# A dense layer's combined weights: made one stage earlier, and the layer's leading pair of tiles by seven block products

## The chip, the cores and the metric

The kernel runs on one core of a Trainium2 chip. That core has a matrix engine (TensorE, PE in the profile), a vector engine (VectorE, DVE), a scalar engine (ScalarE, ACT), a general one (GpSimd, POOL), and a queue engine (SyncE, SP), which issues every DMA of this kernel. Each works through its own list of instructions in order and waits for others on semaphores. The metric is the device time of one execution in microseconds, lower is better, as the median of several executions without the profiler.

## The reference

All data are float32. The input x has two batches of 1024 rows of 1024 numbers. Four residual layers follow one another, each on the layer-normed x:

```
x = x + attn_a(layernorm(x))     # 32 heads, rope, causal, an adapter of 10 keys, output projection w_proj
x = x + ffn(layernorm(x))        # dense 1024x1024 + 8 gated low-rank experts
x = x + attn_b(layernorm(x))     # 8 heads over 1024 keys, not causal, output projection
x = x + ffn(layernorm(x))        # the same dense layer and weights again
```

The dense layer is where the change lies:

```
base_out = x @ W_base.T + b_base
weights  = sparsemax(x @ W_router.T + b_router)        # 8 numbers per row
h        = x @ lora_A                                   # 8 experts x 16
out      = base_out + (h * weights) @ lora_B
```

## The kernel before

A tile is 128 rows of x. A product of two tiles of rows with a 1024x1024 weight can be made plainly, by 32 matmuls of 128x128 by 128x512 (two tiles, two halves of the columns, eight blocks of the inner dimension), or by Strassen's way in Winograd's form: the pair of tiles is one 2x2 matrix of blocks, the weight another, and seven products of blocks take the place of eight. Seven products of four matmuls each are 28. For this the weight's blocks b11, b12, b21, b22 must be combined beforehand (L1294, `combine_weights`): (3) = b22-b12, (2) = (3)+b11, (4) = (2)-b21, and b12 itself is overwritten by b12-b11. Each is a set of four 128x512 pieces, c = 0 to 3. Three sets are kept in DRAM (`tf`) and streamed back through a ring of four places while the layer runs, in the order 2, 3, 4 for every pair of tiles (`piece`, L1238).

The order of the PE's instructions is written out by Python generators, each of which yields after every matmul; the SP's order is written out as well in this part of the kernel. DVE, ACT and POOL are ordered by a scheduler that uses its own costs. Small jobs for the DVE can be put into a queue of chores (`fill.chore`): one is emitted after each matmul, and `fill.flush` emits the rest of a key, with all that stands before it in the queue.

The part of the kernel that the change touches, in the order of time:

1. `proj_a(1, ...)` (L1102): the output projection of the first attention for batch 1, four pairs of tiles, each by seven products (`seven_added`, L1049; products in the order 1, 6, 2, 7, 5, 4, 3, into two PSUM banks that take turns). During it the dense layer's weights are loaded, three DMAs at a time (`each`, L1638). In the last pair the first two tiles of the dense layer are fetched and normalized ahead (`then.prepare()`).
2. `f1_0 = f1(0)`, which is `ffn(b=0, k=0, ...)` (L1201): the first dense layer on batch 0, again four pairs. For each pair: eight transposes per tile (`turn`), `hidden` (16 matmuls of 136 columns per pair, followed on the DVE by the router, `router`, L1241, some 26 small instructions), then the dense product, in whose middle the gated hidden values are transposed (`turned`, L1283, tiles `ht_f` and `hwT`).
3. The first pair of f1_0 is made by `plain` (L1310). Meanwhile `combine_weights` makes the twelve combined pieces on the DVE, in eight places that later serve as ring and work room (`qkb_f`, `kqb_f`), and stores each to `tf`; four more subtractions overwrite b12 ("wb1"). At the end of the pair four pieces are read back into the ring. Pairs 2 to 4 are made by seven products.

The first pair of one later call, `ffn(0, 1, ...)` with `late_room`, is also made by `plain`; that stays.

Of the kernel before, what the change touches and what calls it, by code (L numbers as in the profile page):

```python
# [147 lines left out]
def tile_model(ctx: ExitStack, tc: tile.TileContext, d, out: bass.AP):  # L148
# [950 lines left out]
        return {1: a[11], 2: a[12], 3: a[12], 4: a[22], 5: s1, 6: s2, 7: a[21]}  # L1099


    def proj_a(b, big, wp, tile_of, then=None, each=None):  # L1102

        yts, xs, stores = {}, {}, deque()
        count = {"yt": 0, "x": 0}

        def take(kind, shape, name):
            count[kind] += 1
            return tile_of(kind, count[kind] - 1, shape, name)

        def fetch(p):
            for t in (2 * p + 1, 2 * p):
                yts[t] = take("yt", [P, NG, P], f"yt{b}_{t}")
                for g in range(NG):
                    sp.dma_start(yts[t][:, g, :], yd[b, g][:, t * P : (t + 1) * P])

        def fetch_x(p):
            for t, n in ((2 * p, 0), (2 * p + 1, 1), (2 * p + 1, 0), (2 * p, 1)):
                xs[t, n] = take("x", [P, HF], f"xp{b}_{t}_{n}")
                sp.dma_start(xs[t, n], d["x"][b, t * P : (t + 1) * P, n * HF : (n + 1) * HF])  # L1120

        def store(t, n):
            stores.append((x1[b, t][:, n * HF : (n + 1) * HF], xs.pop((t, n))))
            if len(stores) > 1:
                sp.dma_start(*stores.popleft())

        if not wp:
            for i in range(2):
                wp[i] = big.tile([P, 4, C], F32, tag="h16", name=f"wp{i}")
                for g in range(4):  # L1130
                    sp.dma_start(wp[i][:, g, :], d["w_projT"][(4 * i + g) * P : (4 * i + g + 1) * P, :])
            for i, tag in ((3, "wqk"), (2, "wqk"), (4, "wv")):
                wp["T", i] = big.tile([P, 4, HF], F32, tag=tag, name=f"wpt{i}")
        b11, b12, b21, b22 = (wp[i][:, :, n * HF : (n + 1) * HF] for i in range(2) for n in range(2))
        right = {1: b11, 2: b21, 3: b22, 4: wp["T", 4], 5: b12, 6: wp["T", 2], 7: wp["T", 3]}
        fetch(0)
        fetch_x(0)
        yield READY
        for p in range(NT // 2):
            if then is not None and p == NT // 2 - 1:  # L1140
                then.prepare()
            if p + 1 < NT // 2:
                fetch(p + 1)
            if each is not None:
                each()
            if b == 0 and p == 0:

                for c in range(4):
                    for dst, op, x, y in ((7, pin_sub, b22, b12), (6, pin_add, right[7], b11), (4, pin_sub, right[6], b21)):
                        fill.chore("wp", lambda c=c, dst=dst, op=op, x=x, y=y: op(right[dst][:, c], x[:, c], y[:, c]))  # L1150
                for t in (1, 0):
                    yt = yts.pop(t)
                    for n in range(2):
                        op = next_bank([P, HF], f"op{b}_{t}_{n}")
                        for g in range(NG):
                            mm(op, lhsT=yt[:, g, :], rhs=wp[g // 4][:, g % 4, n * HF : (n + 1) * HF],
                               start=(g == 0), stop=(g == NG - 1))
                            yield HF * COL
                        x = xs[t, n]
                        dve.tensor_add(x, op, x)  # L1160
                        store(t, n)
                    if t == 1:
                        fetch_x(p + 1)
                for c in range(4):
                    fill.chore("wp1", lambda c=c: pin_sub(b12[:, c], b12[:, c], b11[:, c]))
                continue
            nm = f"p{b}_{p}"
            a = {10 * i + j: yts.pop(2 * p + i - 1)[:, 4 * j - 4 : 4 * j] if j == 2 else yts[2 * p + i - 1][:, 4 * j - 4 : 4 * j]
                 for i in (1, 2) for j in (1, 2)}
            left = left_factors(a, *(tile_of("s", i, [P, 4, P], f"s{i}_{nm}") for i in range(2)), nm)  # L1170
            flush = {6: ("wp", nm), 5: ("wp1",)}
            ends = {11: (2 * p, 0), 12: (2 * p, 1), 21: (2 * p + 1, 0), 22: (2 * p + 1, 1)}

            def ready(i):
                for key in flush.get(i, ()):
                    fill.flush(key)
                if i == 2:
                    while stores:
                        sp.dma_start(*stores.popleft())
                    if p + 1 < NT // 2:  # L1180
                        fetch_x(p + 1)
                    elif then is not None:
                        then.prepare()
                if i == 5:
                    if each is not None:
                        each()
                    if then is not None and p == NT // 2 - 1:
                        then.prepare()

            yield from seven_added(nm, left, right, [tile_of("sum", i, [P, HF], f"sum{i}_{nm}") for i in range(2)],  # L1190
                                   {i: xs[at] for i, at in ends.items()}, lambda i: store(*ends[i]), ready)
        sp.dma_start(*stores.popleft())
        yield ("proj", b)
# [2 lines left out]

    tf = {(i, c): dram.tile([P, HF], F32, name=f"tf{i}_{c}") for i in (2, 3, 4) for c in range(4)}

    kept = [{}, {}, {}]

    def ffn(b, k, src, dst, w, wk, tiles, places, free=lambda: True, there=lambda t: True):  # L1201

        tiles = list(tiles)
        first = (b, k) == (0, 0)
        late_room = (b, k, tiles[0]) == (0, 1, 0)

        seq = [t for p in range(0, len(tiles), 2) for t in (tiles[p + 1], tiles[p])]
# [73 lines left out]
        def turned(p):  # L1283
# [4 lines left out]
                flip(tp[:, i, :], hws.pop(t).rearrange("p e r -> p (e r)"), ident)  # L1288
            hwT = wk.tile([P, 4, P], F32, tag="hwT", name=f"hwT_f{b}_{k}_{e}", bufs=1)
            act.copy(hwT[:, :2], tp)  # L1290
            if p or not (first or late_room):
                act.activation(hwT[:, 2], tp[:, 1], AF.Copy, scale=-1.0)
                dve.tensor_sub(hwT[:, 3], hwT[:, 0], hwT[:, 1])
            return hwT  # L1294

        def combine_weights(slots):
            b11, b12, b21, b22 = (w["wb"][:, 4 * i : 4 * i + 4, n * HF : (n + 1) * HF] for i in range(2) for n in range(2))
            ts = {}

            def make(i, c, op, x, y):  # L1300
                t = ts[i, c] = slots[len(ts) % len(slots)]
                op(t, x, y)
                sp.dma_start(tf[i, c], t)

            for c in range(4):
                fill.chore("wb", lambda c=c: make(3, c, pin_sub, b22[:, c], b12[:, c]))
                fill.chore("wb", lambda c=c: make(2, c, pin_add, ts[3, c], b11[:, c]))
                fill.chore("wb", lambda c=c: make(4, c, pin_sub, ts[2, c], b21[:, c]))

        def plain(p):  # L1310
            order = [(n, c) for n in range(2) for c in range(NC)]
            order = order[:4] + order[NC:] + order[4:NC]
            for i in range(2):
                t = seq[2 * p + i]
                ops = {}
                for n, c in order:
# [3 lines left out]
                    op = ops[n]  # L1320
                    mm(op, lhsT=xts[t][:, c, :], rhs=w["wb"][:, c, cols], start=(c == 0), stop=False)
                    yield HF * COL
                    if late_room and (n, c) == (0, 3):

                        pin_add(xs[t][:, HF:], op, xs[t][:, HF:])
                    if (i, n, c) == (0, 0, 3):
                        normalize(2)
                    if late_room and (i, n, c) == (1, 0, 1):
                        while stores:
                            sp.dma_start(*stores.popleft())  # L1330
                        fetch(3)
                    if (i, n, c) == ((1, 1, 5) if late_room else (0, 1, 3)):
                        normalize(3)
                    if i and c == 5:
                        yield from turn(2, (1 - n,))
# [6 lines left out]
                    store(t, n)  # L1342
                    yield HF * COL
            yield from transposed(xns[seq[3]], place_xt(3), f"f{b}_{k}_{seq[3]}", by=(next_bank, next_bank))
            fill.flush("wb")
            if first:
                b11, b12 = (w["wb"][:, :4, n * HF : (n + 1) * HF] for n in range(2))
                for c in range(4):
                    fill.chore("wb1", lambda c=c: pin_sub(b12[:, c], b12[:, c], b11[:, c]))

        def take_room():
            if not room:
                ring, work, more = places()
                room.update(ring=ring, work=work, x=more[:, :2].rearrange("p a c -> p (a c)"),
                            xt=more[:, 2:].rearrange("p a (b c) -> p (a b) c", c=P))
            if not first:
                for c in range(4):
                    piece(2, c)

        fetch(0)  # L1360
        fetch(1)
# [10 lines left out]
        for p in range(n_pairs):  # L1372
# [4 lines left out]
                sp.dma_start(*stores.popleft())  # L1377
            if last:
                yield AHEAD
            plainly = p == 0 and (first or late_room)  # L1380
            if not plainly:
                ring, work = room["ring"], room["work"]
                a = {10 * i + j: xts[t][:, 4 * j - 4 : 4 * j] for i, t in ((1, e), (2, o)) for j in (1, 2)}
# [7 lines left out]
                    if i != 3 or not late_room:  # L1391
                        fetch(i)
            if plainly:
                if first:
                    combine_weights([room[kind][:, c] for kind in ("ring", "work") for c in range(4)])
                yield from plain(p)
                if late_room:
                    while not free():
                        yield WAIT
                    take_room()  # L1400
                else:
                    for c in range(4):
                        piece(2, c)
                continue
            fill.chore(nm, lambda a=a: pin_sub(a[21], a[11], a[21]))
            b11, b12, b21, b22 = (w["wb"][:, 4 * i : 4 * i + 4, n * HF : (n + 1) * HF] for i in range(2) for n in range(2))
# [172 lines left out]
    with tc.manual_schedule(engines={mybir.EngineType.PE}):  # L1579
        with tc.tile_pool(name="big", bufs=2, side="left", reuse_waits="tile") as bigp:  # L1580
# [54 lines left out]
                    return big.tile(shape, F32, tag={"yt": "t4k", "x": "tt"}[kind], name=name)  # L1635
                return pj.tile(shape, F32, tag=kind, name=name)

            fill.add(Dense(lambda: proj_a(1, big, wp, place, f1_0, lambda: load(3))))  # L1638
            fill.drain()
            assert not loads  # L1640
            own.close()
# [105 lines left out]
```

## Time and profile before

| | us |
|---|---|
| median of three executions without the profiler | 2433.34 (2433.07 to 2435.3) |
| the profiled execution, device time | 2443.13 |
| its span, first to last instruction | 2441.4 |
| PE busy in the span | 2377.8 |
| last pair of proj_a(1) on the PE (L198, x_p to z_p) | 1436.72 to 1460.75 |
| transposes of f1_0's first two tiles (L204) | from 1460.75 |
| f1_0: first matmul of `hidden` for pair 1 / pair 2 / pair 3 / pair 4 | 1462.96 / 1506.16 / 1539.56 / 1572.71 |

Times within a trace are microseconds from the start of the span. In a timeline line the first number is the start, the second the length of a merged stretch, x the number of instructions in it. A float32 matmul stands as two records (two passes), so 8 records are one product of four matmuls. Names such as y_p, z_p, x_f are the PSUM banks of the products: _p of the projection, _f of the dense layer; fo_f are the banks of `plain`.

### The profile page before, as it was taken

Reading aid. Unit: us, or ns where it says so; the run is one execution under the profiler, and the core shown is the slowest. Engines: PE = TensorE matmul, PEld = TensorE weight load, DVE = VectorE, ACT = ScalarE, POOL = GpSimd, SP = SyncE. Lnnn points to the kernel's source line nnn. Section 1 sums busy time; section 2 is a strip of 40 time slices with the busy share of each in tenths; the row PEclk is TensorE's granted clock in tenths of the full one; section 3 lists DMA queues with packets and bytes.
Section 4 is the critical chain, followed back from the end, with each engine's and each line's share of the span. In section 5 each row is a group of like instructions: output and inputs, shape, how many; then the busy total and the mean of one; then the engine's idle time right before and its main releaser. Section 6 shows DMA issues by size and latency. Waiting matters only on the chain.

```text
span 2441.4 us, 60572 instructions
## 1 busy us (share of the span) xinstructions
PE 2377.8 (97%) x25147; PEld 1084.3 (44%) x25147; DVE 1429.7 (59%) x4310; ACT 1100.3 (45%) x2104; POOL 591.6 (24%) x927
## 2 busy tenths in 40 slices
PE   8999999999999999999999999999999999989999
PEld 4435443455344544445433444574333643233454
DVE  6576666666656666666741236567666766553453
ACT  2346655666565666566642000013345446654200
POOL 1432222222323223222211131202111112121332
PEclk9999999999999999999999999999999999999999
DMA  4443423333233333333212654532323202123543
GB/s 149 139 131 109 135 88 131 97 93 109 99 111 114 93 97 92 97 97 114 84 62 79 219 182 141 163 123 82 109 87 105 90 25 96 66 95 100 173 156 121
DMA packets 173044, 271.56 MB, mean 111 GB/s; under 512 B 16224, under 2 KB 76768, under 8 KB 172768
## 3 DMA queue, kind: packets, MB, share of 16 engines
q1 hardware_dynamic: 172768, 267.68, 34.2%
q8 instruction: 197, 3.23, 0.5%
q14 instruction: 79, 0.65, 0.1%
HBM read 212.05 MB, written 55.57 MB: 110 GB/s over the span
## 4 chain that ended last, share of the span: by engine, by line
PE 86%; DVE 9%; DMA 2%; ACT 2%; issue 1%; POOL 0%; SPq 0%; DVEq 0%; POOLq 0%
PE st L394 9%; PE sc L322 8%; PE y_A L416 5%; PE y L200 5%; PE y_f L198 4%; PE z L200 4%; PE st L392 3%; PE z_f L198 3%; PE x L200 3%; PE y_v L200 3%; PE x_f L198 3%; PE y_B L416 2%; PE y_f L200 2%; PE y_p L198 2%; DVE pr_A L335 2%; PE x_v L200 2%
## 5 line engine op out<-in xcount | busy, mean ns | idle before, releaser
L506 ACT ACTIVATE pt<-st 128x1024 f32<-128x1024 f32 (+1 forms) x418 | 425.9, 1019 | 615.5 <-PE st L394 484.4
L343 ACT ACTIVATE pr_A<-pr_A,nmax_A 128x896 f32<-128x896 f32 (+7 forms) x512 | 389.9, 765 | 55.1 <-DVE nmax_A L335 54.6
L335 DVE CUSTOM_DVE_ANT_0 pr_A<-sc,mask 128x512 f32<-128x512 f32 (+3 forms) x512 | 251.4, 537 | 193.7 <-PE st L394 92.2
L322 PE MATMUL sc<-kT,qT 32*128 32x512 f32 (+3 forms) x1536 | 328.0, 523 | 3.5 <-DVE part_A L335 1.7
L394 PE MATMUL st<-qT,kT 32*128 32x512 f32 (+3 forms) x1536 | 307.8, 488 | 0.0
L335 DVE CUSTOM_DVE_ANT_0 pr_A<-sc,mask,part_A 128x512 f32<-128x512 f32 (+1 forms) x256 | 156.2, 647 | 147.5 <-PE sc L322 96.7
L401 POOL TENSOR_SCALAR_AFFINE_SELECT pt<-pt 128x256 f32<-128x256 f32 x256 | 106.0, 432 | 470.5 <-ACT pt L506 470.5
L343 ACT ACTIVATE pr_B<-pr_B,nmax_B 128x1024 f32<-128x1024 f32 x128 | 145.6, 1140 | 51.6 <-DVE nmax_B L335 51.6
L239 POOL TENSOR_TENSOR xf<-xf,b_base 128x256 f32<-128x256 f32 x100 | 72.9, 761 | 378.4 <-DVE xn_f L261 330.1
L322 PE MATMUL sc<-kq,qk 32*128 32x512 f32 x512 | 146.8, 650 | 14.1 <-DVE nmax_B L335 9.4
L416 PE MATMUL y_A<-pt,v 128*32 128x512 f32 (+3 forms) x1536 | 158.6, 501 | 0.0
L394 PE MATMUL st<-rows_B,kq 32*128 32x512 f32 x512 | 145.0, 643 | 2.0 <-ACT pt L506 1.4
L394 PEld LDWEIGHTS st<-qT,kT 32*128 32x128 f32 x1536 | 133.8, 185 | 16.6 <-issue 11.6
L392 PE MATMUL st<-rows_A,ones 3*128 3x512 bf16 (+3 forms) x768 | 127.8, 329 | 5.5 <-DVE nmax_A L335 5.0
L335 DVE CUSTOM_DVE_ANT_0 pr_B<-sc,zeros 128x512 f32<-128x512 f32 x128 | 83.3, 687 | 72.4 <-PE sc L322 72.3
L335 DVE CUSTOM_DVE_ANT_0 pr_B<-sc,zeros,part_B 128x512 f32<-128x512 f32 x128 | 91.0, 747 | 58.4 <-PE sc L322 58.4
L392 PEld LDWEIGHTS <-ones 3*128 3x128 bf16 x768 | 36.8, 91 | 196.1 <-issue 188.8
L322 PEld LDWEIGHTS sc<-kT,qT 32*128 32x128 f32 x1536 | 113.5, 184 | 17.9 <-issue 5.9
L830 POOL TENSOR_TENSOR qr<-qr,sin 128x256 f32<-128x256 f32 x64 | 60.5, 945 | 221.5 <-DVE qr L826 220.5
L343 ACT ACTIVATION_READ_ACCUMULATOR pr_A<-pr_A,nmax_A 128x1 f32 x512 | 97.1, 190 | 0.0
L200 PE MATMUL y<-tt,wqk 128*32 128x512 f32 x768 | 92.6, 594 | 0.0
L416 PEld LDWEIGHTS y_A<-pt,v 128*32 128x32 f32 x1536 | 33.8, 109 | 119.9 <-issue 109.2
(429 smaller groups left out, 4227.0 us busy)
## 6 DMA issues: line engine op xcount, KB each, us to landing
tt<-td SPq DMA_DIRECT2D x252, 256.0 KB, 2.8
qkb_f<-tf SPq DMA_DIRECT2D x84, 256.0 KB, 3.0
qkb_s<-tf SPq DMA_DIRECT2D x84, 256.0 KB, 3.1
wqk<-in_w_attnT SPq DMA_DIRECT2D x32, 512.0 KB, 5.2
xf<-x SPq DMA_DIRECT2D x25, 512.0 KB, 4.1
xa<-in_x SPq DMA_DIRECT2D x16, 512.0 KB, 6.0
wv<-in_w_attnT SPq DMA_DIRECT2D x8, 1024.0 KB, 5.4
yd<-ys SPq DMA_DIRECT2D x32, 256.0 KB, 2.7
```

What stands on the lines that cost most here:

```text
L198: return pe.matmul(out, lhsT=lhsT, rhs=rhs, start=start, stop=stop, skip_group_check=True)
L200: pe.matmul(out[i : i + 32], lhsT=lhsT[:, i : i + 32], rhs=rhs, start=start, stop=stop, skip_group_check=True)
L239: pool.tensor_add(dst[:, i : i + 2 * P], a[:, i : i + 2 * P], b[:, i : i + 2 * P])
L322: yield w * COL, lambda: pe.matmul(dst[:, o : o + w], lhsT=self.qt[rows, qc : qc + P], rhs=self.kt[rows, c0 : c0 + w], start=True, stop=True)
L335: minimum[0] = dve.tensor_tensor_reduce(pr[:, c0 : c0 + w], sc[:, i, o : o + w], m, -self.scale, BIG if c0 == 0 else self.part[:, col], AL ...
L343: tc.keep_in_program_order(act.activation(pr[:, :nk], pr[:, :nk], AF.Exp, bias=self.nmax[:, col], scale=-1.0, accum_out=self.sums[:, col]))
L392: yield w * COL / 4, lambda: pe.matmul(dst[:, o : o + w], lhsT=of["ones"][three, :], rhs=self.rows[three, off : off + w], start=True, stop ...
L394: yield w * COL, lambda: pe.matmul(dst[:, o : o + w], lhsT=self.kt[rows, kb * P : (kb + 1) * P], rhs=rhs, start=self.extra, stop=True)
L401: pool.affine_select(out=dg, in_=dg, compare_op=ALU.is_ge, fill=0.0, base=0, pattern=[[0, 2], [1, P]], channel_multiplier=-1)
L416: pe.matmul(self.y[32 * h : 32 * h + 32, off : off + w], lhsT=self.value(h, kb), rhs=pt[h // 2][:, h % 2, o : o + w], start=self.opens, st ...
L506: act.activation(pt[:, :, low_:wide_], st[:, :, low_:wide_], AF.Exp, scale=ts[0][0].scale)
L830: pool.tensor_mul(qr[:, hs], qr[:, hs], sin[:, cols][:, hs])
```

## The change

`combine_weights` becomes a function of its own beside `ffn`, and is called from proj_a(1) at the head of the last pair, through a new argument `meanwhile`. The outstanding store of x is issued first, and four places of the pool that holds the projection's x are taken (`tw0` to `tw3`). The twelve combined pieces pass through these four places in turn, each stored to `tf` from there, so that from the fifth on a piece waits until the store of the one four before it has landed. The four subtractions into b12 follow as chores "wb1". All sixteen stand in the chore queue ahead of the last pair's own left factors, and are emitted by the time of product 6.

In `ffn`, the case `first` is gone: f1_0's leading pair is made by seven products like the others. The ring is filled at its start (`take_room` now issues four reads of `tf` before the pair's own fetches of the tiles of pair 2). `plain` is left for `late_room` alone.

```
@@ proj_a
-    def proj_a(b, big, wp, tile_of, then=None, each=None):
+    def proj_a(b, big, wp, tile_of, then=None, each=None, meanwhile=None):
...
             if each is not None:
                 each()
+            if meanwhile is not None and p == NT // 2 - 1:
+
+                while stores:
+                    sp.dma_start(*stores.popleft())
+                meanwhile([take("x", [P, HF], f"tw{i}") for i in range(4)])
             if b == 0 and p == 0:
...
+    def combine_weights(slots, w):
+
+        b11, b12, b21, b22 = (w["wb"][:, 4 * i : 4 * i + 4, n * HF : (n + 1) * HF] for i in range(2) for n in range(2))
+        ts = {}
+
+        def make(i, c, op, x, y):
+            t = ts[i, c] = slots[len(ts) % len(slots)]
+            op(t, x, y)
+            sp.dma_start(tf[i, c], t)
+
+        for c in range(4):
+            fill.chore("wb", lambda c=c: make(3, c, pin_sub, b22[:, c], b12[:, c]))
+            fill.chore("wb", lambda c=c: make(2, c, pin_add, ts[3, c], b11[:, c]))
+            fill.chore("wb", lambda c=c: make(4, c, pin_sub, ts[2, c], b21[:, c]))
+        for c in range(4):
+            fill.chore("wb1", lambda c=c: pin_sub(b12[:, c], b12[:, c], b11[:, c]))
+
@@ ffn
         tiles = list(tiles)
-        first = (b, k) == (0, 0)
         late_room = (b, k, tiles[0]) == (0, 1, 0)
...
-            if p or not (first or late_room):
+            if p or not late_room:
                 act.activation(hwT[:, 2], tp[:, 1], AF.Copy, scale=-1.0)
                 dve.tensor_sub(hwT[:, 3], hwT[:, 0], hwT[:, 1])
             return hwT
...
@@ plain
             yield from transposed(xns[seq[3]], place_xt(3), f"f{b}_{k}_{seq[3]}", by=(next_bank, next_bank))
-            fill.flush("wb")
-            if first:
-                b11, b12 = (w["wb"][:, :4, n * HF : (n + 1) * HF] for n in range(2))
-                for c in range(4):
-                    fill.chore("wb1", lambda c=c: pin_sub(b12[:, c], b12[:, c], b11[:, c]))
...
@@ take_room
-            if not first:
-                for c in range(4):
-                    piece(2, c)
+            fill.flush("wb")
+            for c in range(4):
+                piece(2, c)
...
-            plainly = p == 0 and (first or late_room)
+            plainly = p == 0 and late_room
...
             if plainly:
-                if first:
-                    combine_weights([room[kind][:, c] for kind in ("ring", "work") for c in range(4)])
                 yield from plain(p)
-                if late_room:
-                    while not free():
-                        yield WAIT
-                    take_room()
-                else:
-                    for c in range(4):
-                        piece(2, c)
+                while not free():
+                    yield WAIT
+                take_room()
                 continue
...
-            fill.add(Dense(lambda: proj_a(1, big, wp, place, f1_0, lambda: load(3))))
+            fill.add(Dense(lambda: proj_a(1, big, wp, place, f1_0, lambda: load(3),
+                                       lambda slots: combine_weights(slots, w))))
```

More of the change, by code (lines that the diff above doesn't have):

```diff
@@ L1294, in turned @@
             return hwT
[L1296 to L1303, printed above, removed]
-            for c in range(4):
-                fill.chore("wb", lambda c=c: make(3, c, pin_sub, b22[:, c], b12[:, c]))
-                fill.chore("wb", lambda c=c: make(2, c, pin_add, ts[3, c], b11[:, c]))
-                fill.chore("wb", lambda c=c: make(4, c, pin_sub, ts[2, c], b21[:, c]))
         def plain(p):
@@ L1322, in plain @@
                     yield HF * COL
-                    if late_room and (n, c) == (0, 3):
+                    if (n, c) == (0, 3):
                         pin_add(xs[t][:, HF:], op, xs[t][:, HF:])
@@ L1327, in plain @@
                         normalize(2)
-                    if late_room and (i, n, c) == (1, 0, 1):
+                    if (i, n, c) == (1, 0, 1):
                         while stores:
@@ L1331, in plain @@
                         fetch(3)
-                    if (i, n, c) == ((1, 1, 5) if late_room else (0, 1, 3)):
+                    if (i, n, c) == (1, 1, 5):
                         normalize(3)
@@ L1393, in ffn @@
             if plainly:
-                if first:
-                    combine_weights([room[kind][:, c] for kind in ("ring", "work") for c in range(4)])
                 yield from plain(p)
-                if late_room:
-                    while not free():
-                        yield WAIT
-                    take_room()
-                else:
-                    for c in range(4):
-                        piece(2, c)
+                while not free():
+                    yield WAIT
+                take_room()
                 continue
```

## Prediction

> **What bounds the kernel now.** I read the page's busy times first, then the PE's timeline over the two stages that change, then the granted clock there, then the DVE's and POOL's timelines, last the DMAs. The page:
>
> ```profile
> span 2441.4 us, 60572 instructions
> PE 2377.8 (97%) x25147; PEld 1084.3 (44%) x25147; DVE 1429.7 (59%) x4310; ACT 1100.3 (45%) x2104; POOL 591.6 (24%) x927
> ```
>
> The PE is the bound: what leaves its list or its waits leaves the time. The PE's timeline, from the projection's last product through f1_0's first pair to the starts of `hidden` for pairs 2, 3 and 4:
>
> ```profile
> 1457.32 3.60 PE L198 MATMUL z_p<-wp,yt 128*128 128x512 f32 x8
> 1460.75 1.04 PE L204 MATMUL xt_f<-ident,xn_f 128*128 128x128 f32 x8
> 1462.96 3.87 PE L198 MATMUL hp_f<-la,xt_f 128*128 128x136 f32 x32
> 1466.67 8.75 PE L198 MATMUL fo_f<-wb,xt_f 128*128 128x512 f32 x20
> 1477.83 0.69 PE L204 MATMUL ht_f<-ident,hs_f 128*128 128x128 f32 x2 [2.42 <-DVE hs_f L1267]
> 1478.31 3.20 PE L198 MATMUL fo_f<-wb,xt_f 128*128 128x512 f32 x4
> ...
> 1487.45 8.85 PE L198 MATMUL fo_f<-wb,xt_f 128*128 128x512 f32 x20 [0.78 <-DVE xf L1341]
> ...
> 1504.83 1.09 PE L204 MATMUL xt_f<-ident,xn_f 128*128 128x128 f32 x8 [0.78 <-DVE xf L1341]
> 1506.16 2.12 PE L198 MATMUL hp_f<-la,vm_f 128*128 128x136 f32 x16 [0.24 <-ACT xt_f L234]
> ...
> 1539.56 2.02 PE L198 MATMUL hp_f<-la,xt_f 128*128 128x136 f32 x16
> ...
> 1572.71 3.87 PE L198 MATMUL hp_f<-la,xt_f 128*128 128x136 f32 x32
> ```
>
> From `hidden` to `hidden`, the plain pair takes 1506.16 - 1462.96 = 43.20, the pairs by seven products 33.40 (to 1539.56) and 33.15 (to 1572.71). Eight records of 512 columns take 3.43 from start to start (1457.32 to 1460.75), so one matmul is 0.858. The four records at 1478.31 took 3.04 until the next group at 1481.35, where 1.72 is usual: the clock was down behind the idle 2.42. The same place by stretches of four us (span, busy PE, PEld, DVE, ACT, POOL, then granted clock, DMA share, GB/s):
>
> ```profile
> 1472.00:1476.00 4.00, 3.41 (x8) 1.15 (x7) 4.00 (x13) 0.00 (x0) 2.83 (x4) 1.00 0.05 18
> 1476.00:1480.00 4.00, 2.17 (x4) 1.16 (x5) 4.00 (x10) 0.60 (x3) 0.96 (x1) 0.69 0.40 149
> 1480.00:1484.00 4.00, 4.00 (x10) 1.79 (x9) 2.85 (x7) 0.18 (x1) 0.04 (x1) 0.88 0.68 249
> ```
>
> The DVE is full from 1472 to 1480 and the clock sags after the PE's gap. On the DVE, the router's small steps (they end in `hs_f`, which the PE waits for) stand between the twelve combinations; and a combination that meets POOL takes 1.07 where 0.69 is usual. The DVE's line before that is from the projection's last pair:
>
> ```profile
> 1443.86 0.69 DVE L227 TENSOR_TENSOR sum_p<-sum_p,y_p 128x512 f32<-128x512 f32 x1 [4.16 <-PE y_p L198]
> ...
> 1474.18 1.07 DVE L224 TENSOR_TENSOR kqb_f<-wb 128x512 f32<-128x512 f32 x1
> ...
> 1475.30 1.08 DVE L227 TENSOR_TENSOR kqb_f<-kqb_f,wb 128x512 f32<-128x512 f32 x1
> ```
>
> ```profile
> 1473.17 3.79 POOL L239 TENSOR_TENSOR xf<-xf,b_base 128x256 f32<-128x256 f32 x4 [12.36 <-DVE xn_f L261]
> ```
>
> And the DMAs, issue to landing (KB each, median us), within 1395 to 1515:
>
> ```profile
> x<-xp SPq DMA_DIRECT2D x13, 256.0 KB, 3.2
> xf<-x SPq DMA_DIRECT2D x5, 512.0 KB, 4.3
> tf<-qkb_f SPq DMA_DIRECT2D x8, 256.0 KB, 2.0
> ```
>
> **The change part by part.** *The leading pair by seven products.* The plain pair's 43.20 becomes that of a pair by seven products: 33.15 or 33.40 in the rows, I take 33.3, so **-9.9** (ends -10.05 and -9.8). Of 10.05, four matmuls fewer are 4 x 0.858 = 3.43; the idle 2.42 and the 1.32 of low clock behind it are 3.74; two waits of 0.94 for bank reads by the DVE at L1341 and 0.45 of transposes that nothing covers at the pair's end are 2.3; the rest, 0.6, is smaller gaps. The added copies, sums, the third and fourth hwT block and the POOL additions are in the 33.3 already, since pairs 2 to 4 have them. The seven products need their left sums at product 6; in the changed DVE list these come directly after the transposes' copies, some 5 us ahead.
>
> *Sixteen DVE instructions in the projection's last pair.* At 0.60 from start to start, they are 9.6. Between 1440 and 1460 the DVE was busy 9.7 of 20, so they fit, but just. I walked the changed DVE list: four of them run right after 1437.6, the rest from the sum of product 6 (1443.75, PE's end of y_p) on, with one or two between any two instructions that the PE waits for. By 0.60 a step I get the read of x_p's bank at 1449.1 (product 5 wants it at 1450.45), the sum of product 7 at 1452.5 (product 4 wants its bank at 1453.89), product 3's left factor at about 1456 (wanted at 1457.32), the first normalized tile at 1457.7 (wanted 1460.75) and the second between 1460 and 1461.5 (wanted 1461.8 by its transposes). The last has next to no margin, and POOL's pieces decide it: six pieces of POOL's additions run among these sixteen. DVE additions beside POOL that read a PSUM bank kept their 0.69 (1454.14, 1457.59), those with both inputs in SBUF took 0.84 (1448.61), 1.07 and 1.08; the sixteen are of the latter kind. A meeting costs 0.15 to 0.38, six of them 0.9 to 2.3, of which some 0.4 is margin. Ends 0 (no meeting) and +1.9; I take **+1.0**, the middle, since 0.84 is from this very stretch and 1.07 from a denser one.
>
> The Trainium skill speaks against the change here: its page SBUF — State Buffer, section Who interferes with whom, says that a VectorE instruction with two SBUF inputs and a GpSimd one that reads SBUF exclude each other for their whole length. By that rule the sum is worse: the price is under rival 2.
>
> *Their places.* A place of `tw` comes back after four combinations, 3.5 to 6 us in my walk; the store from it lands after 2.0 to 3.2 (rows). Cost 0, covered by the combinations between; the SP issues them with nothing urgent behind (the projection's stores, then f1_0's reads). The first four pieces wait for stores of the third pair's x, the last issued at 1437.64; its place is wanted at 1444.4.
>
> *The SP's list at the start of f1_0.* Four ring reads now stand ahead of the fetches of pair 2's tiles (1462.04 and 1462.56 before). Four such reads took 1.83 to issue at 1500.55, and the projection's last store ahead of them waits for a DVE addition that comes some 0.5 later: the fetch goes out at about 1464.6, and 1 MB stands before it. At 254 to 337 GB/s (stretches in which the queues were full) that is 3 to 4, so the ring is filled by 1468.5, wanted at 1470.1, and the fetched tile lands between 1469 and 1471. Its batch-norm statistics stand in the changed DVE list ahead of the router's last two steps; the DVE gets there at 1470.3 (copy at 1466.9, about 3.4 of small steps, as at 1543.47 to 1549), needs 1.8 more, and the PE wants `hs_f` at 1473.5. Free up to a landing at 1471.7: cost **0**, ends 0 and +3.7 (the gap that it would reopen, 2.42 and its 1.3 of low clock).
>
> *Pair 2.* It no longer has the plain pair's tail before it: 33.40 to 33.15 at best, I count 0 (end -0.25).
>
> Sum: -9.9 + 1.0 = **-8.9**. The profiled execution (2443.13: span 2441.4 and 1.7 around it) becomes 2434.2. The median without the profiler is 9.8 lower; the PE is as full on either side of this place, so I carry the difference over: 2433.34 - 8.9 = **2424.4**. Everything behind f1_0 has the same instructions in the same order on all engines, and the PE's chain runs through it, so it moves forward as a whole.
>
> **The rivals.**
>
> 1. *The router's gap stays*: the tile fetched behind the ring reads lands after 1471.7 (longest landing of a ring transfer in the trace: 6.4), and the PE stands again before the `ht_f` transposes. A full return is 2.4 + 1.3: gain 5.2, 2428.1. The page TensorE: Matmul & The Clock Gate of the Trainium skill (What's actually happening) lets the clock fall after an idle window of about 3.4 us; by it the 1.3 would not come, but here an idle of 2.42 was followed by a granted 0.69.
> 2. *The DVE becomes the bound in the projection's last pair*: each of six POOL pieces (0.69 alone: 2.77 for four) holds the DVE for its whole length, 4.2 - 0.4 margin = 3.8 at the transposes: gain 6.1, 2427.2; with low clock behind it 2428.5. For it speak 1.07 and 1.08, against it that even these are 0.38 and not a whole piece of 0.69. The page on SBUF, in full, gives this case.
> 3. *The four places strangle it* (the other sign): the chain of places runs through the DVE, which does nothing else while it waits. The twelfth combination needs two landings after 1445.1, then product 3's factor: 1446.6 + 2L against 1457.3. With L = 5 nothing is lost; slower than before from 2L - 10.7 = 9.9, L of 10.3 us on, at L = 12 by 3.4 (2436.7). Rows say 2.0 to 3.2, DMA share in 1440 to 1460 was 0.06 to 0.16.
> 4. *No change that counts*: the gain is eaten further on, for instance by a fetch that comes no earlier: 2433. Against it: all weights are loaded by then.
>
> **How the numbers follow.** Forecast 0.71, from 2422.8 (-10.3 with pair 2, and 0.2 for the spread of the runs) to 2425.8; rival 1 0.11; rival 2 0.09; rival 3 0.05; rival 4 0.04. Range 2422.0 to 2428.5: the forecast, and rivals 1 and 2 for the most part; 0.8 more below for the spread of three runs. A measurement of this kernel tells 0.2%, 4.9 us, from no change: faster is below 2428.5. Faster: 0.71 + 0.10 + 0.05 = 0.86; same: 0.02 + 0.03 + 0.04 = 0.09; slower 0.05.
>
> **What the profile after would show.** Right: from `hidden` of pair 1 to that of pair 2 about 33.3, with no idle before `ht_f` and clock 1.00; no fo_f in that stretch; the projection's last pair still 24 on the PE and at most 1 idle at the second tile's transposes. Wrong: idle before `ht_f` (rival 1), idle in the last pair's products or its transposes with the DVE full (2), DVE waits of `tw` on DMA (3).

## The result, and the profile after

The changed kernel took 2428.48 us (median of 12 executions, 2423.42 to 2432.91); the kernel before, on the same chip, took 2436.11 (12 executions, 2433.07 to 2439.52). The ratio is 0.9967, with a 95% interval of 0.9959 to 0.9975. That is 8.0 us less of 2436 (6.1 to 10.0), against a forecast of 8.9 less. The first two lines of the page after:

```profile
span 2427.2 us, 60606 instructions
PE 2367.8 (98%) x25139; PEld 1081.3 (45%) x25139; DVE 1432.7 (59%) x4317; ACT 1100.8 (45%) x2106; POOL 599.3 (25%) x933
```

The PE has eight records fewer, which are the four matmuls that the eighth product of blocks had. The two profiled spans differ by 14.2, more than the change is worth, so the span isn't the place to read it. The PE's timeline of the kernel after, over the projection's last pair and f1_0's pairs (start, length, instructions; in brackets the idle time before):

```profile
1434.40 3.60 PE L198 MATMUL x_p<-wp,yt 128*128 128x512 f32 x8
...
1448.14 3.60 PE L198 MATMUL z_p<-wp,s_p 128*128 128x512 f32 x8
1451.57 3.60 PE L198 MATMUL y_p<-wpt,yt 128*128 128x512 f32 x8
1456.27 3.70 PE L198 MATMUL z_p<-wp,yt 128*128 128x512 f32 x8 [1.10 <-DVE ve_f L251]
1459.80 1.04 PE L204 MATMUL xt_f<-ident,xn_f 128*128 128x128 f32 x8
...
1462.01 3.87 PE L198 MATMUL hp_f<-la,xt_f 128*128 128x136 f32 x32
1465.72 3.60 PE L198 MATMUL x_f<-wb,xt_f 128*128 128x512 f32 x8
...
1472.59 0.38 PE L204 MATMUL ht_f<-ident,hs_f 128*128 128x128 f32 x2
...
1495.16 2.02 PE L198 MATMUL hp_f<-la,vm_f 128*128 128x136 f32 x16
...
1528.31 2.02 PE L198 MATMUL hp_f<-la,xt_f 128*128 128x136 f32 x16
```

Three lengths cover the whole stretch that changed: from the projection's last pair (first x_p line) to `hidden` of pair 1, from there to `hidden` of pair 2, and on to that of pair 3. The last pair starts at 1436.72 before and at 1434.40 after.

| us | before | after | change |
|---|---|---|---|
| last projection pair's start to `hidden` of pair 1 ("lead-in") | 26.24 | 27.61 | +1.37 |
| `hidden` of pair 1 to that of pair 2 | 43.20 | 33.15 | -10.05 |
| pair 2 to pair 3 | 33.40 | 33.15 | -0.25 |
| sum | 102.84 | 93.91 | **-8.93** |

The rest of the 14.2 lies where both kernels have the same work: 2.32 ahead of the stretch (the starts above) and some 3.0 behind it, from `hidden` of pair 3 to the end (901.84 before, 898.89 after). Other profiled executions of this study took 895.9 to 899.9 for that last part and reached the stretch at 1434.2 to 1435.0: it differs from run to run, and the profiled execution of before was a long one.

The idle time before `ht_f` is gone, and the clock no longer falls in the pair (1.00 in each stretch of four us from 1464 to 1484). What came in is the 1.10 before the projection's last product. From start to start it costs 1.27: the product begins 4.70 after the one ahead of it, where 3.43 is usual. The product itself then takes 3.53 to the first transposes, which makes up the +1.37 of the lead-in. The DVE's timeline of the kernel after around that wait:

```profile
1443.94 1.22 DVE L224 TENSOR_TENSOR wb<-wb 128x512 f32<-128x512 f32 x1
...
1452.01 1.02 DVE L224 TENSOR_TENSOR yt<-yt,s_p 128x512 f32<-128x512 f32 x1
...
1453.02 0.68 DVE L244 BATCH_NORM_STATS2 stats_f<-xf 128x6 f32<-128x512 f32 x1
...
1453.74 0.68 DVE L244 BATCH_NORM_STATS2 stats_f<-xf 128x6 f32<-128x512 f32 x1
1454.34 1.21 DVE L261 TENSOR_SCALAR xn_f<-xf,mv_f,r_f 128x1024 f32<-128x1024 f32 x1
...
1455.59 0.63 DVE L1065 TENSOR_TENSOR xp<-xp,z_p 128x512 f32<-128x512 f32 x1
1456.14 0.14 DVE L251 TENSOR_SCALAR ve_f<-mv_f 128x1 f32<-128x1 f32 x1
```

The last but one, L1065, reads the bank z_p that product 5 has filled; it ends at 1456.22, and the PE starts at 1456.27. The PE's bracket names `ve_f`, the next small instruction of the DVE, which product 3 doesn't use. The weight load that goes ahead of product 3 names the read itself (waits of the kernel after from 1434 to 1465: total, times, longest):

```profile
PEld z_p L198 <- DVE xp L1065: 1.9, 1, 1.9
```

`seven_added` says why the PE needs it. Product 3 adds into the same bank, without a new start:

```
in_halves(x[22], x[22], s1)
...
yield from product(5, z, stop=False)
ends(22, dve.tensor_add, z)
...
yield from product(3, z, start=False)
```

So result 22 has to be read out after product 5 and before product 3. (The first line is one of POOL's additions: the read adds onto the same rows of x and has to come behind it, too.) The DVE's list is full from 1442 to 1456.8, without an idle stretch, and in that list the first tile's normalization (L261) and the second tile's statistics (L244) stand ahead of this read. Three instructions of the list took longer beside POOL's additions, whose timeline is this:

```profile
1442.36 2.25 POOL L220 TENSOR_TENSOR xp<-xp,sum_p 128x256 f32<-128x256 f32 x2 [14.46 <-DVE sum_p L227]
1450.23 4.76 POOL L220 TENSOR_TENSOR xp<-xp,sum_p 128x256 f32<-128x256 f32 x4 [5.62 <-issue]
```

The same engines in the kernel before, DVE and then POOL:

```profile
1452.21 1.25 DVE L261 TENSOR_SCALAR xn_f<-xf,mv_f,r_f 128x1024 f32<-128x1024 f32 x1
1454.14 0.69 DVE L1065 TENSOR_TENSOR xp<-xp,z_p 128x512 f32<-128x512 f32 x1 [0.69 <-PE z_p L198]
```

```profile
1444.68 1.41 POOL L220 TENSOR_TENSOR xp<-xp,sum_p 128x256 f32<-128x256 f32 x2 [14.46 <-DVE sum_p L227]
...
1452.18 3.22 POOL L220 TENSOR_TENSOR xp<-xp,sum_p 128x256 f32<-128x256 f32 x4 [0.78 <-POOL xf L239]
```

There the read of z_p waited for the PE and not the PE for the read, and one normalization took 1.25 beside POOL without harm.

The clock of the kernel after in the same place, in stretches of four us (span, busy PE, PEld, DVE, ACT, POOL, granted clock, DMA share, GB/s):

```profile
1448.00:1452.00 4.00, 4.00 (x11) 1.71 (x9) 4.00 (x9) 0.41 (x2) 1.77 (x1) 1.00 0.64 242
1452.00:1456.00 4.00, 3.17 (x8) 1.14 (x6) 4.00 (x9) 0.00 (x0) 3.37 (x5) 1.00 0.40 153
1456.00:1460.00 4.00, 3.73 (x10) 1.77 (x11) 2.24 (x7) 0.41 (x2) 4.00 (x6) 1.00 0.35 131
```

The clock stays at 1.00 through the wait and behind it, so the wait costs the 1.27 and the 0.10 named above, and no slower matmuls behind it.

### The profile page after: what moved, and what is told of

Same layout as the page of the kernel before. It is cut to its first block, busy times and chain, and to the rows that moved or that the text cites. A ratio compares the mean times of both kernels' runs of the same rounds, so it can differ in the third digit from the quotient of the medians.

```text
span 2427.2 us, 60606 instructions
## 1 busy us (share of the span) xinstructions
PE 2367.8 (98%) x25139; PEld 1081.3 (45%) x25139; DVE 1432.7 (59%) x4317; ACT 1100.8 (45%) x2106; POOL 599.3 (25%) x933
## 3 DMA queue, kind: packets, MB, share of 16 engines
q8 instruction: 197, 3.23, 0.6%
## 4 chain that ended last, share of the span: by engine, by line
PE 87%; DVE 9%; ACT 2%; DMA 1%; issue 1%; POOL 0%; SPq 0%; DVEq 0%
PE st L394 9%; PE sc L322 8%; PE y_A L416 5%; PE y L200 5%; PE y_f L198 4%; PE z_f L198 4%; PE z L200 4%; PE st L392 3%; PE x_f L198 3%; PE x L200 3%; PE y_v L200 3%; PE y_B L416 2%; PE y_f L200 2%; DVE pr_A L335 2%; PE y_p L198 2%; PE x_v L200 2%
```

## The experiments

Each table entry below is read as above, in us; "sum" runs from the last projection pair's start to `hidden` of pair 3, and "wait" is the idle time before product 3.

| kernel | lead-in | pair 1 to 2 | pair 2 to 3 | sum | against before | wait |
|---|---|---|---|---|---|---|
| before | 26.24 | 43.20 | 33.40 | 102.84 | | none |
| changed, profiled again | 27.61 | 33.15 | 33.15 | 93.91 | -8.93 | 1.10 |
| combinations early, pair 1 plain | 26.24 | 39.04 | 33.58 | 98.86 | -3.98 | none |
| changed, POOL's sums left out | 26.32 | 33.15 | 33.15 | 92.62 | -10.22 | none |
| changed, "wb1" in f1_0's pair 1 | 26.24 | 33.16 | 33.15 | 92.55 | -10.29 | none |
| changed, second tile prepared later | 26.24 | 33.15 | 33.15 | 92.54 | -10.30 | none |
| changed, two places | 29.07 | 33.25 | 33.15 | 95.47 | -7.37 | 1.03 |

**The changed kernel once more.** No edit.

> The changed kernel once more, so that the others of this group can be set beside it on one chip. Both theories: the ratio to the kernel before stays near 0.9967. In the trace, the lead-in (start of the last projection pair's product 1 to the first hidden matmul of f1_0's pair 1) is about 27.6 us against 26.24 before, hidden of pair 1 to hidden of pair 2 is 33.15 against 43.20, and the wait of about 1.1 to 1.3 us stands before the last projection pair's product 3.

Measured: 2428.29 (median of 6) against 2437.93 (17 of before), ratio 0.996, interval 0.9947 to 0.9974. All three local lengths came back to the hundredth, the wait too. What the stretch gives is thus a property of the kernel; the totals scatter by more.

**The combinations early, the leading pair left plain.** One half of the change alone: against the kernel before, `combine_weights` moves into the projection's last pair, without the "wb1" subtractions, which stay at the plain pair's end.

```
+                meanwhile([take("x", [P, HF], f"tw{i}") for i in range(4)])
...
-                if first:
-                    combine_weights([room[kind][:, c] for kind in ("ring", "work") for c in range(4)])
                 yield from plain(p)
```

> One part alone: the twelve combinations are made in the projection's last pair, but f1_0's leading pair stays plain (the four subtractions into b12 stay at its end). Theory (the plain pair lost 3.7 us to combinations standing between the router's steps, and 3.43 to four matmuls): hidden to hidden falls from 43.20 to about 39.0 = 33.15 + 3.43 + two bank waits of 0.94 + 0.45 of uncovered transposes; no gap before the ht_f transposes; lead-in 26.2 to 27.0. Gain 3.5 to 4.2, ratio about 0.9984. Rival (the plain order itself makes the gaps, the combinations are innocent): hidden to hidden stays above 42, gain below 1, ratio 1.000, and the whole gain of the change is the seven products.

Measured: 2435.40 (median of 11) against 2437.93, ratio 0.9991 (0.9982 to 0.9999), that is 2.2 less (0.2 to 4.4). The interval holds the 3.98 of the stretch and the 3.5 to 4.2 that were expected, but the totals alone would not show so much. Its PE timeline in f1_0's leading pair:

```profile
1461.07 3.87 PE L198 MATMUL hp_f<-la,xt_f 128*128 128x136 f32 x32
1464.78 8.75 PE L198 MATMUL fo_f<-wb,xt_f 128*128 128x512 f32 x20
1473.36 0.38 PE L204 MATMUL ht_f<-ident,hs_f 128*128 128x128 f32 x2
1473.58 1.88 PE L198 MATMUL fo_f<-wb,xt_f 128*128 128x512 f32 x4
...
1481.39 8.85 PE L198 MATMUL fo_f<-wb,xt_f 128*128 128x512 f32 x20 [0.78 <-DVE xf L1347]
...
1498.77 1.09 PE L204 MATMUL xt_f<-ident,xn_f 128*128 128x128 f32 x8 [0.79 <-DVE xf L1347]
1500.11 2.12 PE L198 MATMUL hp_f<-la,vm_f 128*128 128x136 f32 x16 [0.24 <-ACT xt_f L234]
```

The `ht_f` line has no bracket: the router was in time, as soon as the combinations did not stand between its steps. The four records behind it take 1.72 until the next line, not 3.04, and the clock is 1.00 from 1464 to 1480. The two waits for bank reads are still there, since they belong to the plain order. So taking the combinations out is worth 43.20 - 39.04 = 4.16, and the seven products, by difference, the remaining 39.04 - 33.15 = 5.89.

**POOL's sums left out.** Against the changed kernel, this one leaves out POOL's six additions of sums onto x in the projection's last pair, so those rows of x lack them:

```
-        in_halves = in_pieces(pool.tensor_add)
+        in_halves = in_pieces(pool.tensor_add) if halves else (lambda *_: None)
...
+                                   halves=meanwhile is None or p < NT // 2 - 1)
```

> Leaves out POOL's additions of the sums onto x in the last projection pair (so that pair's rows are without them); all else as in the changed kernel. Theory A (meetings of VectorE with POOL are the price: three VectorE instructions were 0.34 to 0.54 us longer, 1.28 in all, before the read of product 5's bank): the wait before product 3 falls from 1.27 to 0.4 or less, lead-in 26.3 to 26.7. Theory B (the sixteen instructions by their number are the price): the wait stays at 0.9 or more, lead-in 27.2 or more.

Measured: one execution, 2424.55. The wait is gone. Its DVE timeline (two lines), then its PE timeline (one):

```profile
1451.37 0.69 DVE L224 TENSOR_TENSOR yt<-yt,s_p 128x512 f32<-128x512 f32 x1
...
1454.17 0.64 DVE L1065 TENSOR_TENSOR xp<-xp,z_p 128x512 f32<-128x512 f32 x1
```

```profile
1454.90 3.67 PE L198 MATMUL z_p<-wp,yt 128*128 128x512 f32 x8
```

The read of z_p comes 19.87 after the pair's start (1434.30), in the changed kernel 21.19: 1.32 earlier. The three long DVE instructions are back at their lengths: 1.22, 1.02 and 1.21 became 0.69, 0.69 and 0.80, together 1.27 of the 1.32. The DVE's instructions up to the read and their order are those of the changed kernel. So without POOL's sums the wait goes: with this list, the length that they add to the three is what makes the read late.

**"wb1" later.** Against the changed kernel, the four subtractions into b12 go into f1_0's leading pair, behind the router's last multiplication.

```
-        for c in range(4):
-            fill.chore("wb1", lambda c=c: pin_sub(b12[:, c], b12[:, c], b11[:, c]))
...
+            if (b, k, p) == (0, 0, 0):
+                for c in range(4):
+                    fill.chore("wb1", lambda c=c: behind(dve.tensor_sub(w["wb"][:, c, HF:], w["wb"][:, c, HF:], w["wb"][:, c, :HF])))
```

> The four subtractions into b12 move from the projection's last pair to f1_0's leading pair, behind the router's last step (product 5 is the first to read them); the twelve combinations stay where the change put them. Theory (the wait before product 3 is VectorE running late by sixteen instructions): four fewer are 2.4 us, more than the wait of 1.27, so it goes; lead-in 26.24 to 26.5; hidden to hidden stays 33.15 to 33.4 since VectorE stands idle 2 to 4 us there; 1.0 to 1.3 us faster than the changed kernel, ratio to before about 0.996. Rival (they only move the lateness): product 5 or product 7 of f1_0's pair waits for VectorE, hidden to hidden 34.2 or more, no gain over the changed kernel.

Measured: 2427.26 (median of 5) against 2437.93, ratio 0.9957 (0.9945 to 0.9969). Four DVE instructions fewer in front of the read are enough for the wait to go, and pair 1 pays nothing for them (33.16). Its DVE timeline there:

```profile
1469.32 0.29 DVE L1293 TENSOR_TENSOR hs_f<-hs_f,z_f 128x128 f32<-128x128 f32 x1
1469.52 1.89 DVE L1409 TENSOR_TENSOR wb<-wb 128x512 f32<-128x512 f32 x3
```

**The same work in another order.** The three runs so far took work away from the DVE's list or made it cheaper. This one leaves all of it and moves one request: the second tile's normalization is asked for at product 4 and not, as in the changed kernel, at product 5. (The products run 5, 4, 3, so that is one product later.)

```
                 if i == 5:
                     if each is not None:
                         each()
-                    if then is not None and p == NT // 2 - 1:
-                        then.prepare()
+                if i == 4 and then is not None and p == NT // 2 - 1:
+                    then.prepare()
```

> The changed kernel with one thing moved: the second tile of f1_0 is normalized from product 4 of the projection's last pair on, not from product 5, so that VectorE's list has its two batch-norm statistics behind the read of product 5's bank and no longer ahead of it. The same sixteen instructions, the same POOL work. Theory (product 3 adds into the bank that product 5 filled and so waits until VectorE has read it; the place of that read in VectorE's list decides, 1.9 us of work go behind it): the wait before product 3 goes from 1.27 to at most 0.2, the second tile is normalized just in time, lead-in 26.24 to 26.6. Rival (VectorE is late by its whole load): the wait moves to the second tile's transposes, lead-in stays 27.2 to 27.8.

Measured: 2426.98 (median of 6) against 2437.51 (9), ratio 0.9961 (0.9949 to 0.9974). The wait is gone and nothing took its place at the transposes (lead-in 26.24). Its DVE timeline, then its PE timeline:

```profile
1451.85 1.02 DVE L224 TENSOR_TENSOR yt<-yt,s_p 128x512 f32<-128x512 f32 x1
...
1453.49 0.69 DVE L1065 TENSOR_TENSOR xp<-xp,z_p 128x512 f32<-128x512 f32 x1 [0.56 <-POOL xp L220]
...
1454.22 0.68 DVE L244 BATCH_NORM_STATS2 stats_f<-xf 128x6 f32<-128x512 f32 x1
1454.82 0.80 DVE L261 TENSOR_SCALAR xn_f<-xf,mv_f,r_f 128x1024 f32<-128x1024 f32 x1
```

```profile
1454.84 3.60 PE L198 MATMUL z_p<-wp,yt 128*128 128x512 f32 x8
```

Now the read comes first, and behind it come the second tile's statistics and also the first tile's L259 and L261, which the scheduler moved along; POOL's four additions still take 4.76. So the wait isn't for want of DVE time: it is the place of one read in a list that has room further on. The read's bracket shows its other condition: it waited 0.56 for POOL's addition onto the same rows, and still ended at 1454.18, ahead of product 3.

Each of these runs thus removes the wait by another means: four subtractions fewer, three shorter instructions, or another order. It was a deadline missed by 1.2 us to which all three contributed, and none of them is the cause alone.

**Two places instead of four.**

```
-                meanwhile([take("x", [P, HF], f"tw{i}") for i in range(4)])
+                meanwhile([take("x", [P, HF], f"tw{i}") for i in range(2)])
```

> Two places for the twelve combinations in place of four, all else as in the changed kernel; each combination now waits for the store two before it. Stores land 2.0 to 3.3 us after their issue. Theory (the places are covered by the work between): VectorE shows waits on these stores of 0.5 to 1.5 us each for some six combinations, but none stands ahead of what the matrix engine wants; lead-in 26.3 to 27.6, not above the changed kernel's. Rival (the landing times strangle VectorE, rival 3 of the prediction): the wait before product 3 or the transposes grows by 2 us or more, lead-in above 29.5.

Measured: one execution, 2429.42; lead-in 29.07, outside both expectations. No DVE instruction on `tw` waited for a store. But the scheduler, given other buffers, gave DVE and POOL another order. The DVE's timeline, POOL's and the PE's:

```profile
1455.40 0.69 DVE L1065 TENSOR_TENSOR xp<-xp,z_p 128x512 f32<-128x512 f32 x1 [3.23 <-POOL xp L220]
```

```profile
1449.73 4.27 POOL L239 TENSOR_TENSOR xf<-xf,b_base 128x256 f32<-128x256 f32 x4 [5.57 <-DVE xn_f L261]
1453.97 2.76 POOL L220 TENSOR_TENSOR xp<-xp,sum_p 128x256 f32<-128x256 f32 x4
```

```profile
1456.14 3.70 PE L198 MATMUL z_p<-wp,yt 128*128 128x512 f32 x8 [1.03 <-DVE ve_f L251]
...
1462.82 0.44 PE L204 MATMUL xt_f<-ident,xn_f 128*128 128x128 f32 x2 [1.20 <-DVE xp L1065]
```

POOL now makes the first tile's bias additions before its sums, and the read of z_p adds onto what POOL's sum has to deliver first: the DVE stands for 3.23, and all of its list behind it. Since the order changed as well, the run is no clean test of landings, for which it was meant; it says again that this read is where the stage can break.

## Why the prediction was right, and where it was not

**The sum.** Forecast -8.9, the stretch gave -8.93, the medians -7.6 and the ratio -8.0 (6.1 to 10.0). The absolute 2424.4 was made on a median of 2433.34; in the comparison the kernel before itself stood at 2436.11, which is 2.8 of the 4.1 by which 2428.48 lies above it, and 1.3 is the difference between 8.9 and 7.6. 2428.48 also lies above the forecast's own part of the range, which ended at 2425.8: it stands where the range had room for rivals 1 and 2, and 0.02 below its end of 2428.5. That the absolute time held is therefore luck; what held by its working is the difference. The near agreement of -8.9 with -8.93 is partly luck too, as the terms show.

**The leading pair, -9.9.** Right: -10.05, the end of its range, since the pair took 33.15. The composition held in its two main parts. The combinations between the router's steps (idle 2.42 and low clock 1.32, forecast 3.74) gave 4.16 when they alone were taken out. The seven products gave 5.89: four matmuls by 0.858 are 3.43, and 2.46 is what the plain order loses, where the forecast's two waits, uncovered transposes and the rest made 2.3 and 0.6. The 0.4 too little on the one side is the 0.4 too much on the other.

**Sixteen DVE instructions, +1.0.** Right in size (+1.37), wrong in place. The walk through the changed DVE list gave good times: shifted by the 2.32 that the after run is ahead, it puts the end of product 3's left factor at 1453.7 (measured 1453.03), the first normalized tile at 1455.4 (1455.55) and the second between 1457.7 and 1459.2 (1458.34). What failed is its list of deadlines: "product 3's left factor at about 1456 (wanted at 1457.32)" was the only thing that it had product 3 wait for. The read of product 5's bank was missing from it. Shifted, that was wanted at 1455.0 and ended at 1456.22: 1.2 late, and the wait stands there and not at "the second tile's transposes", which did not wait. The meetings with POOL were mis-sized as well: three long ones of 0.54, 0.34 and 0.40 (1.28 together), where the forecast had six of 0.15 to 0.38. Not all of the 1.28 is new: two instructions of the same kind were long in the kernel before, 0.84 (1448.61) and 1.25 (1452.21), by 0.16 and 0.44. The sum of the errors happened to stay within its ends of 0 and +1.9. That the price hung on the order, and could be zero with the same sixteen instructions, was shown only by the run that moved one step.

**Their places, 0.** Right. The stores from `tw` landed soon, and no combination waited for one. The kernel after, DMA issues from 1435 to 1453 (KB each, median us to landing):

```profile
tf<-tw SPq DMA_DIRECT2D x12, 256.0 KB, 2.0
```

**The SP's list, 0.** Right. DMA issues of the kernel after from 1461 to 1464, and then its DVE timeline:

```profile
qkb_f<-tf SPq DMA_DIRECT2D x4, 256.0 KB, 4.6
xf<-x SPq DMA_DIRECT2D x1, 512.0 KB, 5.6
```

```profile
1469.13 0.68 DVE L244 BATCH_NORM_STATS2 stats_f<-xf 128x6 f32<-128x512 f32 x1
...
1470.46 0.27 DVE L1287 TENSOR_TENSOR hs_f<-hs_f,z_f 128x128 f32<-128x128 f32 x1
```

The fetch was issued at 1463.00 and landed 5.6 later, at 1468.6; the DVE got to it at 1469.13 without a wait, and `hs_f` was done at 1470.73, 1.86 ahead of the `ht_f` transposes at 1472.59. What a landing later than that slack would cost was not tried.

**Pair 2, 0.** -0.25, the end named.

**The rivals.** The router's gap (1) did not stay. The places did not strangle the DVE (3): no combination waited for a store, with four places or, in another order, with two. That nothing counts (4) is excluded by the interval. The DVE as the bound by exclusion with POOL (2) had the right parties, and the sign that the prediction gave for it did come: idle time among the last pair's products with the DVE full, and 25.40 on the PE for that pair, not 24. But its size was 1.27 and not 3.8, it was not at the transposes, and the exclusion was one condition among three: without it the read came 1.32 earlier, and with it but in another order nothing waited. The Trainium skill's page SBUF — State Buffer (Who interferes with whom) has one of the two block for the other's whole instruction. The traces agree in kind: three DVE instructions grew by 0.34 to 0.54, each less than one POOL piece (0.69), and POOL's four pieces grew from 2.77 to 4.76. A whole piece per meeting, which rival 2 took from that rule, was not reached in any of the three. Nor did each meeting cost the DVE: POOL's first piece of the four took 2.26, from 1450.23 on, and the DVE's subtractions at 1450.62 and 1451.23 beside it kept 0.68.

**What stays open.** The order with the second tile prepared later is 1.37 shorter in the stretch than the change as made, and the one with "wb1" later 1.36. That is 0.06% of the whole, and the intervals of the totals (0.9949 to 0.9974 and 0.9945 to 0.9969, against 0.9947 to 0.9974 for the changed kernel) overlap, so in the totals they are not told apart.

## What to carry to other kernels

When work moves into a stage that has room, list for every instruction of the PE what must have been written and what must have been read before it; a bank that a second product adds into has to be read out in between, by another engine, and that deadline doesn't show in the second product's factors. Then look at the order: here work of the normalization ahead of such a read cost 1.37 us, though the DVE is busy only 59% over the kernel, and the same work behind the read cost nothing. And split a gain by a run that makes one half of the change: here 4.2 of 10 us came from the router's steps, freed of the work between them, and not from the saved matmuls.

## What the runs showed that was not expected

- A short wait left the clock alone: behind 1.27 us from start to start the granted clock was 1.00, where the kernel before had 0.69 and 0.88 in the two stretches that hold and follow its idle 2.42.
- A TENSOR_SCALAR with one tensor in SBUF (128x1024) also lost to POOL: 1.21 beside its additions, 0.80 to 0.81 without them. The forecast had counted only additions with both inputs in SBUF, though the trace of before has the same instruction at 1.25 beside POOL (1452.21).
- Both sides lose: in the pair with the combinations POOL's four additions took 4.76 and its two 2.25, where the kernel before shows 3.22 and 1.41 for the same.
- Fewer buffers changed the order and not the waits for the buffers: with two places the scheduler put POOL's bias additions first, and the DVE stood 3.23 for a sum that POOL made later.
